# Products of all row elements, 1 core: the input loaded as seven units ahead and nine in one mid-run transfer, in place of seven loads spread over the start and mid-run

## The chip, the cores and the metric

The kernel runs on one core of a Trainium2 chip. The metric is the device time in microseconds (us), median of several executions. Before the change it is 1261.65 us, the median of 3 runs (1261.52 to 1261.91).

## What is computed

For each of 4096 rows of 256 float32 values, all products of two elements of the row with the second index not below the first, 32,896 values a row:

```
def reference(r_inputs):                       # (4096, 256) float32
    dot = jnp.einsum('bi,bj->bij', inputs, inputs)
    iu, ju = jnp.triu_indices(256)
    return dot[:, iu, ju]                      # (4096, 32896) float32
```

The output has 539 MB, the input 4.2 MB: the kernel writes 128 times what it reads.

## The kernel before, in words

**Tiles.** The 4096 rows lie on 128 partitions, 32 consecutive rows on each. Two rows of every partition make a *unit* (2 KB a partition, 256 KB in all), so the input has 16 units, numbered 0 to 15, and all of it stays in one tile `x`. A unit's output is cut into three parts of 10,944 to 11,008 columns; one part of one unit is a *piece*, 48 in all, written by one store of some 11 MB. `PASS = 6` pieces (two units) make a pass; the loop variable `h` counts the 8 passes and `p` the piece within a pass. Pieces 0 and 1 are made ahead of the loop, by VectorE with ScalarE (`scalar`, line 297) and, for piece 1, GpSimd.

**Stages.** Two output places `o` are used in turn (`PLACES = 2`). For each piece VectorE (`vector`, line 225; L275) makes most of the products, each instruction one or two runs of consecutive columns for both rows, and GpSimd (`gpsimd`, line 341; L360) the last part, up to an estimated 19.4 us (`BUDGET`). VectorE's first instruction of a piece waits until the store of the piece two before has landed (`free`), and releases GpSimd (`go`); its last one waits for GpSimd (`g_done`) and releases the store (`v_done`). SyncE (`sync`, line 380; L392) issues the stores in order, all on one queue. At the first piece of each unit VectorE copies the unit from `x` to `xv` and `xp` (L252, L254), from which both engines then read.

**The head.** Piece 0 is stored in five parts (`FIRST`, cuts at columns 704, 1984, 3968 and 6592), each as soon as ScalarE (L303) and VectorE (L236) have made it, so that stores begin early. TensorE only waits until all five have landed, then hands the place on (line 447).

**Loads.** SyncE issues three ahead of everything (lines 429 to 432): unit 0, then units 3, 4, 7 and 8 in one transfer, then unit 12. GpSimd issues the rest. Once unit 0 is there it loads units 1, 2, 5 and 6 (`EARLY`) in four transfers of 42, 42, 42 and 2 partitions, combed over the partitions (lines 438 to 445). In pass `h = 2`, after its part of piece `p = 2`, that is the fifteenth piece, it loads units 9 to 11 and 13 to 15 (`LATE`) in transfers of 100, 3 and 25 partitions (`late`, line 329); at `p = 5` of that pass it waits for them. Between these loads stand *marks*: transfers of 256-byte pieces of so many input rows (`STEPS`, `SKIP`) to a tile `marks` that nothing reads. What they have to do with the loads is worked out in the prediction.

## Time and profile before

| what | value |
|---|---|
| median of 3 runs | 1261.65 us |
| the profiled execution, its own time | 1261.66 us |
| its span (first to last instruction) | 1259.9 us |
| VectorE, GpSimd, ScalarE busy | 792.5, 800.1, 27.1 us |
| DMA: moved, mean rate | 543.25 MB, 431 GB/s |
| SyncE's queue / GpSimd's queue | 540.54 MB / 2.64 MB |
| DMA packets under 512 B | 1466 of 15,847 |

How to read it. The profile shows the DMA engines of the core as one line of tenths and one of GB/s; the transfer records behind it list every packet with its start, its duration, its size and its queue, but not the engine that carried it. An instruction's idle time stands before it, with what ended that idle time. The profiled execution's own time agrees with the median of the runs within 0.01 us, and lies 1.76 us above its span.

### The profile page before, as it was taken

Reading aid. Unit: us, or ns where it says so; the run is one execution under the profiler, and the core shown is the slowest. Engines: PE = TensorE matmul, PEld = TensorE weight load, DVE = VectorE, ACT = ScalarE, POOL = GpSimd, SP = SyncE. Lnnn points to the kernel's source line nnn. Section 1 sums busy time; section 2 is a strip of 40 time slices with the busy share of each in tenths; the row PEclk is TensorE's granted clock in tenths of the full one; section 3 lists DMA queues with packets and bytes.
Section 4 is the critical chain, followed back from the end, with each engine's and each line's share of the span. In section 5 each row is a group of like instructions: output and inputs, shape, how many; then the busy total and the mean of one; then the engine's idle time right before and its main releaser. Section 6 shows DMA issues by size and latency. Waiting matters only on the chain. (4 is left out here: it accounts for less than half of the span.)

```text
span 1259.9 us, 2787 instructions
## 1 busy us (share of the span) xinstructions
DVE 792.5 (63%) x1256; ACT 27.1 (2%) x74; POOL 800.1 (64%) x1124
## 2 busy tenths in 40 slices
DVE  8656746667475674766647666486655866468560
ACT  8000000000000000000000000000000000000000
POOL 7477674776666766477665775567656676566750
DMA  9999999999999999999999999999999999999999
GB/s 375 441 427 441 429 437 431 434 434 434 436 433 428 435 435 431 435 428 438 430 438 430 439 428 438 430 438 431 434 436 431 437 431 436 429 436 429 440 428 395
DMA packets 15847, 543.25 MB, mean 431 GB/s; under 512 B 1466, under 2 KB 1504, under 8 KB 3296
## 3 DMA queue, kind: packets, MB, share of 16 engines
q1 hardware_dynamic: 14704, 540.54, 99.3%
q0 software_dynamic: 1136, 2.64, 0.6%
q14 instruction: 7, 0.06, 0.0%
HBM read 4.21 MB, written 538.97 MB: 431 GB/s over the span
## 5 line engine op out<-in xcount | busy, mean ns | idle before, releaser
L360 POOL TENSOR_TENSOR o<-xv 128x696 f32<-128x696 f32 (+33 forms) x1105 | 791.1, 756 | 416.8 <-DVE o L275 416.5
L275 DVE TENSOR_TENSOR o<-xv,xp 128x588 f32<-128x588 f32 (+4 forms) x1195 | 761.1, 712 | 430.3 <-DMA out_dram<-o 195.3
L303 ACT ACTIVATE o<-x 128x198 f32<-128x198 f32 (+34 forms) x72 | 25.5, 447 | 0.8 <-DMA x<-in_r_inputs_dram 0.8
L254 DVE COPY xp<-x 128x512 f32 x15 | 10.3, 688 | 0.0
L236 DVE TENSOR_TENSOR o<-x,xp 128x470 f32<-128x470 f32 (+18 forms) x19 | 9.7, 585 | 0.0
L236 DVE TENSOR_TENSOR o<-x 128x510 f32<-128x510 f32 (+9 forms) x10 | 5.7, 646 | 2.5 <-DMA x<-in_r_inputs_dram 2.5
L252 DVE COPY xv<-x 128x512 f32 x15 | 6.4, 427 | 0.5
L327 POOL DMA_DIRECT2D x<-in_r_inputs_dram x7 | 4.5, 649 | 1.6 <-DMA x<-in_r_inputs_dram 1.6
L321 POOL DMA_DIRECT2D marks<-in_r_inputs_dram x6 | 3.6, 602 | 1.2 <-SPq L175 1.2
L346 POOL MEMSET xv<- 128x1 f32 x1 | 0.1, 93 | 2.1 <-POOLq L188 2.1
L435 ACT ACT_TABLE_LOAD x1 | 1.3, 1283 | 1.2 <-ACTq L188 1.2
L433 DVE MEMSET edge<- 128x32 f32 x1 | 0.1, 85 | 1.0 <-SPq L175 1.0
L232 DVE COPY xp<-x 128x512 f32<-128x512 f32 x1 | 0.7, 684 | 0.0
L347 POOL COPY xv<-x 128x512 f32<-128x512 f32 x1 | 0.6, 609 | 0.0
L435 ACT ACTIVATE edge<-edge 128x1 f32<-128x1 f32 x1 | 0.3, 296 | 0.0
L471 POOL MEMSET const-float32-0.0<- 128x1 f32 x1 | 0.1, 98 | 0.2 <-issue 0.2
L471 POOL MEMSET const-bfloat16-1.0<- 128x1 bf16 x1 | 0.1, 101 | 0.0
L471 POOL MEMSET const-uint8-127<- 128x1 uint8 x1 | 0.1, 101 | 0.0
L471 POOL MEMSET const-float32-1.0<- 128x1 f32 x1 | 0.1, 98 | 0.0
## 6 DMA issues: line engine op xcount, KB each, us to landing
out_dram<-o SPq DMA_DIRECT2D x31, 10944.0 KB, 32.9
out_dram<-o SPq DMA_DIRECT2D x16, 11008.0 KB, 31.2
out_dram<-o SPq DMA_DIRECT2D x1, 4352.0 KB, 18.6
out_dram<-o SPq DMA_DIRECT2D x1, 2624.0 KB, 13.8
out_dram<-o SPq DMA_DIRECT2D x1, 1984.0 KB, 11.8
out_dram<-o SPq DMA_DIRECT2D x1, 1280.0 KB, 9.9
x<-in_r_inputs_dram POOLq DMA_DIRECT2D x1, 1200.0 KB, 39.7
x<-in_r_inputs_dram SPq DMA_DIRECT2D x1, 1024.0 KB, 5.2
```

The costliest lines, as they stand in the source:

```text
L232: nc.vector.tensor_copy(xp, x_of(h, 0)).then_inc(v_own, 1)
L236: ins = nc.vector.tensor_tensor(place[:, :, at - lo : at - lo + length], window(x_of(h, 0)[:, j:], [[d, REPEAT], [1, 1], [1, length]]), wi ...
L252: ins = nc.vector.tensor_copy(xv[:, :each], x_of(h, p // PIECES))
L254: nc.vector.tensor_copy(xp, x_of(h, p // PIECES)).then_inc(v_own, 1)
L275: ins = nc.vector.tensor_tensor(place[:, :, at : at + m * length], window(xv[:, j:], [[d, REPEAT], [1, m], [1, length]]), window(xp[:, i:] ...
L303: nc.scalar.activation(places[p][:, r, at - lo : at - lo + length], xa[:, r * d + j : r * d + j + length], AF.Copy, scale=xa[:, r * d + i ...
L321: nc.gpsimd.dma_start(marks[lo:hi, :, :MARK], of).then_inc(marked, 16)
L327: nc.gpsimd.dma_start(to, of).then_inc(far, 16)
L347: nc.gpsimd.tensor_copy(xv[:, :each], x_of(0, 0)).then_inc(g_own, 1)
L360: ins = nc.gpsimd.tensor_tensor(place[:, :, at : at + m * length], window(xv[:, j:], [[d, REPEAT], [1, m], [1, length]]), window(xv[:, i:] ...
L435: nc.scalar.activation(edge[:, :1], edge[:, 1:2], AF.Copy, scale=edge[:, 2:3])
L471: nc = _bacc.Bacc("TRN2", target_bir_lowering=False, num_devices=1)
```

## The change

SyncE now loads unit 0 in two transfers, one for each of a partition's two rows, and then units 1 to 6 in one transfer of 12 KB a partition. GpSimd loads nothing at the start. In pass `h = 2`, ahead of its part of piece `p = 5` (the eighteenth piece), it issues a mark of 5 rows, a load of units 7 to 15 for partitions 0 to 119, a mark of 2 rows, and the same load for partitions 120 to 127: 18 KB a partition. It waits for them ahead of piece `p = 2` of pass 3. Since the first half of unit 0 can be there alone, VectorE's first instruction is split by row, and ScalarE does the first block row by row; each engine's first instruction on the second row waits for the second half. The counters that GpSimd and VectorE keep are carried on between the two halves of a pass in one way for both. The core of the diff:

```diff
-NEAR = [(0, 1, 1), (3, 7, 2), (12, 13, 1)]
-EARLY = (1, 5, 2)
-LATE = (9, 13, 3)
-WHEN = 2
-BEGUN, HAD = 2, 5
+NEAR = (1, 2, 3)
+LATE = (7, 3, 3)
+BEGUN, HAD = (2, 5), (3, 2)
-COMB = 3
-STEPS = (5, 2, 2, 12, 4)
-TENS, ODD, SKIP = 100, 3, 13
+MOST = 120
+STEPS = (5, 2)
...
-                    for i, j, at, length in block:
+                    todo = [(run, 0, REPEAT) for run in block]
+                    if c == 0:
+                        todo[:1] = [(block[0], r, 1) for r in range(REPEAT)]
+                    for (i, j, at, length), r, rows in todo:
...
+                        if r:
+                            ins._wait_ge(loaded[r], 16)
...
+                if p == c == 0:
+                    for r in range(1, REPEAT):
+                        todo[[of for _, of in order].index(r)]._wait_ge(loaded[r], 16)
...
     def late(h, p: int):
-        with nc.gpsimd.If(h == WHEN):
-            if p == BEGUN:
-                load(LATE, slice(0, TENS))
-                load(LATE, slice(TENS, TENS + ODD))
-                mark(0, SKIP)
-                load(LATE, slice(TENS + ODD, P))
-            else:
-                nc.gpsimd.wait_ge(far, 16 * (COMB + 4))
-                nc.gpsimd.wait_ge(marked, 16 * (COMB + 3))
+        if p == BEGUN[1]:
+            with nc.gpsimd.If(h == BEGUN[0]):
+                at = 0
+                for step, rows in zip(STEPS, (slice(0, MOST), slice(MOST, P))):
+                    mark(at, at + step)
+                    at += step
+                    to, of = units(LATE, rows)
+                    nc.gpsimd.dma_start(to, of).then_inc(far, 16)
+        if p == HAD[1]:
+            with nc.gpsimd.If(h == HAD[0]):
+                nc.gpsimd.wait_ge(far, 16 * len(STEPS))
+                nc.gpsimd.wait_ge(marked, 16 * len(STEPS))
                 nc.gpsimd.drain()
...
-    for (one, two, units), sem in zip(NEAR, loaded):
-        dims = [[(two - one) * each, 2 if two - one > units else 1], [1, units * each]]
-        to, of = (window(ap[:, one * each :], dims) for ap in (flat, x_in))
-        nc.sync.dma_start(to, of).then_inc(sem, 16)
+    for r in range(REPEAT):
+        part = slice(r * d, (r + 1) * d)
+        nc.sync.dma_start(flat[:, part], x_in[:, part]).then_inc(loaded[r], 16)
+    nc.sync.dma_start(*units(NEAR, slice(0, P))).then_inc(loaded[REPEAT], 16)
...
-    at = 0
-    for k, step in enumerate(STEPS):
-        if k == 1:
-            nc.gpsimd.wait_ge(loaded[0], 16)
-        if k:
-            load(EARLY, slice(k - 1, k + COMB * (teeth - 1), COMB) if k <= COMB else slice(P - rest, P))
-        mark(at, at + step)
-        at += step
-
+    nc.gpsimd.wait_ge(loaded[0], 16)
+    nc.gpsimd.wait_ge(loaded[1], 16)
```

More of the change, by code (lines that the diff above doesn't have):

```diff
@@ L181 @@
     head, v_done, a_done, go = (semaphore(s) for s in ("head", "v_done", "a_done", "go"))
-    loaded = [semaphore(f"loaded{k}") for k in range(len(NEAR))]
+    loaded = [semaphore(f"loaded{k}") for k in range(REPEAT + 1)]
     far, marked = semaphore("far"), semaphore("marked")
-    teeth = P // COMB
-    rest = P - COMB * teeth
     def take(engine, sem, value: int):
@@ L234, in vector @@
                         copied = done
-                    for i, j, at, length in block:
+                    todo = [(run, 0, REPEAT) for run in block]
+                    if c == 0:
+                        todo[:1] = [(block[0], r, 1) for r in range(REPEAT)]
+                    for (i, j, at, length), r, rows in todo:
+                        left = xp if c >= DIRECT else x_of(h, 0)
                         ins = nc.vector.tensor_tensor(
-                            place[:, :, at - lo : at - lo + length],
-                            window(x_of(h, 0)[:, j:], [[d, REPEAT], [1, 1], [1, length]]),
-                            window(xp[:, i:] if c >= DIRECT else x_of(h, 0)[:, i:], [[d, REPEAT], [1, 1], [0, length]]),
+                            place[:, r : r + rows, at - lo : at - lo + length],
+                            window(x_of(h, 0)[:, r * d + j :], [[d, rows], [1, 1], [1, length]]),
+                            window(left[:, r * d + i :], [[d, rows], [1, 1], [0, length]]),
                             ALU.mult,
                         )
+                        if r:
+                            ins._wait_ge(loaded[r], 16)
                         if copied:
@@ L300, in scalar @@
         for p in pieces:
-            for _, _, block, _, lo in blocks(p, True):
+            for c, (_, _, block, _, lo) in enumerate(blocks(p, True)):
+                order = [(run, r) for run in block for r in range(REPEAT)]
+                if p == c == 0:
+                    order.sort(key=lambda of: of[1])
                 todo = [
@@ L308, in scalar @@
                     )
-                    for i, j, at, length in block
-                    for r in range(REPEAT)
-                ]
+                    for (i, j, at, length), r in order
+                ]
+                if p == c == 0:
+                    for r in range(1, REPEAT):
+                        todo[[of for _, of in order].index(r)]._wait_ge(loaded[r], 16)
                 if todo:
@@ L321, in mark, with units, gpsimd @@
         nc.gpsimd.dma_start(marks[lo:hi, :, :MARK], of).then_inc(marked, 16)
-    def load(of_units: tuple, rows: slice):
-        one, two, units = of_units
-        dims = [[(two - one) * each, 2], [1, units * each]]
-        to, of = (window(ap[rows, one * each :], dims) for ap in (flat, x_in))
-        nc.gpsimd.dma_start(to, of).then_inc(far, 16)
-    def late(h, p: int):
-        with nc.gpsimd.If(h == WHEN):
-            if p == BEGUN:
-                load(LATE, slice(0, TENS))
-                load(LATE, slice(TENS, TENS + ODD))
-                mark(0, SKIP)
-                load(LATE, slice(TENS + ODD, P))
-            else:
-                nc.gpsimd.wait_ge(far, 16 * (COMB + 4))
-                nc.gpsimd.wait_ge(marked, 16 * (COMB + 3))
+    def units(of_units: tuple, rows: slice) -> tuple:
+        one, parts, of_part = of_units
+        dims = [[of_part * each, parts], [1, of_part * each]]
+        return tuple(window(ap[rows, one * each :], dims) for ap in (flat, x_in))
+    def late(h, p: int):
+        if p == BEGUN[1]:
[10 more added lines that the diff above has]
+                nc.gpsimd.wait_ge(marked, 16 * len(STEPS))
                 nc.gpsimd.drain()
-    def gpsimd(h, pieces: range, ahead: bool):
-        done = turns = 0
+    def gpsimd(h, pieces: range, ahead: bool, done: int = 0, turns: int = 0) -> tuple:
         if ahead:
@@ L353, in gpsimd @@
             turns += not ahead
+            if not ahead:
+                late(h, p)
             order = interleave(block)
@@ L373, in gpsimd @@
             ins.then_inc(g_done, 1)
-            if p in (BEGUN, HAD) and not ahead:
-                late(h, p)
-        nc.gpsimd.sem_inc(g_own, -done)
-        if turns:
-            nc.gpsimd.sem_inc(go, -turns)
+        return done, turns
     def sync():
@@ L396, in sync, with settle @@
             nc.sync.sem_inc(sem, -count)
-    def settle(counts: tuple):
-        for sem, count in zip((v_own, g_done), counts):
-            nc.vector.sem_inc(sem, -count)
+    def settle(engine, counts: tuple):
+        for sem, count in zip((v_own, g_done) if engine is nc.vector else (g_own, go), counts):
+            if count:
+                engine.sem_inc(sem, -count)
     def all_pieces(engine, pieces_of):
-        by_vector = engine is nc.vector
-        counts = pieces_of(0, range(AHEAD), True)
-        if by_vector:
-            settle(counts)
-        for sem in loaded[1:]:
-            engine.wait_ge(sem, 16)
-        engine.wait_ge(far, 16 * (COMB + 1))
-        engine.wait_ge(marked, 16 * (COMB + 2))
+        settle(engine, pieces_of(0, range(AHEAD), True))
+        engine.wait_ge(loaded[REPEAT], 16)
         kind = engine.engine
@@ L420, in all_pieces @@
                 nxt = nc.s_assert_within(h + 1, 0, passes - 1)
-                if by_vector:
-                    settle(vector(nxt, range(AHEAD), False, *counts))
-                else:
-                    pieces_of(nxt, range(AHEAD), False)
-        if by_vector:
-            nc.vector.wait_ge(v_own, counts[0]).then_inc(v_done, 1)
-            settle(counts)
-    for (one, two, units), sem in zip(NEAR, loaded):
-        dims = [[(two - one) * each, 2 if two - one > units else 1], [1, units * each]]
-        to, of = (window(ap[:, one * each :], dims) for ap in (flat, x_in))
-        nc.sync.dma_start(to, of).then_inc(sem, 16)
+                settle(engine, pieces_of(nxt, range(AHEAD), False, *counts))
+        if engine is nc.vector:
+            nc.vector.wait_ge(v_own, counts[0]).then_inc(v_done, 1)
+        settle(engine, counts)
+    for r in range(REPEAT):
+        part = slice(r * d, (r + 1) * d)
+        nc.sync.dma_start(flat[:, part], x_in[:, part]).then_inc(loaded[r], 16)
+    nc.sync.dma_start(*units(NEAR, slice(0, P))).then_inc(loaded[REPEAT], 16)
     nc.vector.memset(edge, 0.0).then_inc(warm, 1)
```

## The prediction

> **What bounds the kernel now.** I read the page's busy shares, its slices and its DMA queues first.

> ```profile
> DVE 792.5 (63%) x1256; ACT 27.1 (2%) x74; POOL 800.1 (64%) x1124
> DMA  9999999999999999999999999999999999999999
> q1 hardware_dynamic: 14704, 540.54, 99.3%
> q0 software_dynamic: 1136, 2.64, 0.6%
> ```

> No engine is over 64% busy; the DMA engines are full in every slice. By stretches (second column: length in us; last two: DMA share, GB/s):

> ```profile
> 0.00:2.00 2.00, 0.09 (x1) 0.78 (x1) 0.60 (x5) 1.00 0.03 3
> 2.00:4.00 2.00, 0.36 (x1) 1.16 (x3) 0.42 (x2) 1.00 0.92 298
> 6.00:8.00 2.00, 2.00 (x4) 2.00 (x7) 2.00 (x4) 1.00 0.98 318
> 430.00:1240.00 810.00, 518.07 (x821) 0.00 (x0) 521.37 (x739) 1.00 1.00 434
> ```

> The first packet runs at 1.98 us; from there to the end something is always moving. The waits agree: the compute engines wait for stores or for each other, with room.

> ```profile
> POOL o L360 <- DVE o L275: 416.5, 46, 12.6
> DVE o L275 <- DMA out_dram<-o: 195.3, 31, 9.1
> ```

> So the time is the start (2 us), the work of the most loaded of 16 DMA engines, and its idle time. Only those three can move it. The transfer records show the work: a packet is followed by the next 4 ns before its recorded end, so I can follow each engine from packet to packet. Every store closes with 16 four-byte completions, one per engine. Their times, relative to the first (us):

> ```
> piece 1  : 0.00 1.11 1.24 1.28 1.33 1.38 1.49 1.59 1.68 1.73 1.81 1.87 1.96 2.14 2.29 2.70
> piece 12 : 0.00 0.04 0.04 0.09 0.14 0.24 0.35 0.44 0.49 0.52 0.57 0.63 0.72 0.90 1.05 1.86
> piece 15 : 0.00 1.79 2.81 2.86 2.91 3.56 3.61 3.65 3.68 3.76 3.83 3.87 3.96 4.00 4.08 4.14
> piece 47 : 0.00 1.02 1.06 1.12 1.77 1.82 1.86 1.89 1.97 2.04 2.08 2.16 2.21 2.25 2.29 2.35
> ```

> The last engine ends 0.61 us after the mean of piece 47: perfect balance would gain only that. Three engines are odd. One **drifts**: 1.24 us ahead of the pack's front at piece 1, level at 12, ahead by 2.81 after the late load, 1.2 behind the same neighbours at 47; that is 0.11 to 0.126 us a store, about 5.9 us in all (its packets are stretched by 4 to 33 ns now and then). Two others, A and B, lose about 2.05 and 1.3 us before piece 12, around six of the 8 KB instruction packets (queue 14) between 31 and 140 us.

> **The rule.** [...] of the 256 late packets of 6144 bytes, the chains that I can follow cleanly carry 20 or 21, one none, as 100 rows on ten engines give. [...] From cursor 0, before: mark 5 moves it to 5, each load of 42 rows takes 14 engines (3 rows each) and leaves out 3 and 4; late, 100 rows take 5 to 14 (10 rows each), 3 rows take 15, 0, 1, mark 13 passes over 2 to 14, 25 rows take 15, 0 to 3 (5 rows each). Engine 4 gets no GpSimd load and 3 and 2 little: the drifter is 4, the one with most lead at piece 15; A is 3 and B 2, which fits the 1.79 (A) and a level B. Afterwards: mark 5, then 120 rows on 15 engines, 8 rows each, leaving out 4; mark 2 passes 4 and 5; 8 rows fall on 6 to 13. So 4 gets nothing, 0 to 3, 5, 14, 15 eight rows, 6 to 13 nine.

> **Prices.** Net per packet (recorded less 4 ns): 2 KB 80 ns, 4 KB 155, 6 KB 230. The line through these gives 43 ns for 1 KB, 455 for 12 KB, 680 for 18 KB. Bounds for 18 KB: the same slope (680), or three packets of 6 KB (690): 0.1 us over nine rows. For 1 KB: 43 to 80, 0.6 us over 16.

> **Part by part, on one engine.**
> 1. SyncE's loads: before 16x80 + 16x155 = 3.76 us; after 16x43 + 8x455 = 4.32 (+0.56).
> 2. Early GpSimd loads, gone: 3 transfers x 3 rows x 2 x 155 = 2.79 us on the full engines.
> 3. Late load: before 20x230 = 4.60; after nine rows 6.12, or eight 5.44.
> 4. Marks and completions of GpSimd's 13 transfers: about 0.3 us; of 4, about 0.1.

> Full engine before: 3.76+2.79+4.60+0.3 = 11.45. After, 6 to 13: 4.32+6.12+0.1 = 10.54 (-0.91). Engine 3 (A): 4.32+5.44+0.1+2.05 = 11.91 (**+0.46**); no early load is withheld from it any more. Engine 2: 11.16. Drifter: 4.32+0.1+5.9 = 10.32. So A ends last.

> 5. Idle at the start. Early loads covered it: the trace shows two engines without them (3 and 4) idle from 6.75 to 7.21 and from 8.95 to 9.56 us, waiting for the first two head stores, which were issued at 4.83 and 6.69 and first moved 2.4 and 2.9 us later. Afterwards all 16 are like these two. But their loads end 0.56 later (7.3), and the head is earlier: half of unit 0 is issued at the same 0.96, has half the bytes, and lands by about 3.2 instead of 3.64; the second, issued some 0.45 later, by about 3.5. VectorE's first instruction (cadence 0.61) becomes two of 0.34, hidden under those waits; then store 1 can go at about 4.4. If the second half lands late (4.1), store 1 goes at 5.0. New idle time: between 0 (stores early) and 1.05 (the whole idle time of those two engines); between the two halves another 0 to 0.2. I take 0.2.
> 6. A's place in the pack: the ten full engines end spread over 0.6 us and the last counts; A alone takes a middle place: -0.3.
> 7. GpSimd's four issues (2.5 us from 364.40 to 367.06 now) move before the eighteenth piece, into the 8.64 us that it waits there anyway; before, they stood in a wait of 9.35.

> ```profile
> 364.40 1.43 POOL L327 DMA_DIRECT2D x<-in_r_inputs_dram  x2
> 366.39 0.67 POOL L327 DMA_DIRECT2D x<-in_r_inputs_dram  x1
> 376.41 18.21 POOL L360 TENSOR_TENSOR o<-xv 128x924 f32<-128x924 f32 x14 [9.35 <-DVE o L275]
> 431.02 14.71 POOL L360 TENSOR_TENSOR o<-xv 128x292 f32<-128x292 f32 x39 [8.64 <-DVE o L275]
> ```

> Behind them on GpSimd stands only that piece; SyncE's queue shares engines, not instructions. The load gets a packet in turn with a store packet (8 x 2.3 = 18 us) and has until the twenty-second piece, some 100 us. The wait for it at piece 2 of pass 3 finds it landed: nothing. The wait for units 1 to 6, ahead of the loop, too.
> 8. Stores are issued some 3.7 us before an engine runs dry (issue 451.11, its first packet 1.0 later, pieces of 25.8 us). The drifter, freed of loads, would lead A by about 5.8 and is stopped at 3.7; with 29 stores x 0.12 = 3.5 still to lose it ends about level with A. No cost, but no reserve either.

> Sum: +0.46 +0.2 -0.3 = +0.4 us on the profiled execution (1261.66; the median is the same within 0.01): **1262.0 us**. A measurement of this kernel tells some 0.2% (2.5 us) from no change, so I call this no change.

> **Rivals.**
> - *The instruction packets fall elsewhere or at other times* (the program is shorter), so that A is no outlier. Then 6 to 13 end last: -0.91+0.2 = -0.7: **1260.9**. For: nothing ties those packets to engine 3 but one trace. Against: the engines' loops stay as they are. 28 in 100.
> - *The head stores come late and all engines idle* as the two did: +0.46+1.05-0.1 = **1263.1**. For: the same wait is in the trace. Against: the stores should come 0.4 earlier and the loads last 0.56 longer. 13 in 100.
> - *The skipped place isn't the drifter's.* If 120 rows are dealt otherwise (16 engines, or another cursor), the drifter carries eight or nine rows: 4.32+5.44+5.9+0.1 = 15.8, +4.3 against 11.45, +0.2: **1266.1**, slower. It decides from the sixth row on the drifter. For: [...] engine numbers aren't recorded. Against: the same walk explains who leads at piece 15. 6 in 100.
> - *Faster by more than 0.2%*: mean work falls only from 10.24 to 9.83 us an engine (all load packets over 16), and 0.61 of imbalance is there; 1.0 together. 2 in 100.

> The forecast has 49; 2 remain for a slowdown that I don't see. Range 1260.4 to 1263.8: it takes in the forecast, the first two rivals and the bounds of steps 1 and 5. Faster 0.02, within 0.2% 0.90, slower 0.08.

> **What would show it.** Records: 256 packets of 1 KB (near 46 ns), 128 of 12 KB (near 460) and 128 of 18 KB (near 684); no GpSimd DMA before 360 us; four issues near 422 us and no longer idle time ahead of the next VectorE piece. Completions at the last piece: one engine last, alone, by about 1.4 us, and the drifter near it. First store issued near 4.4. It is wrong if some engine ends over 2 us after the others (the cursor), if slices after the first fall below 427 GB/s (stores dry), or if the first slice falls below 370 (idle start).

## The result, and the profile after

| | median, us | ratio to before, 95% interval |
|---|---|---|
| before | 1261.61 (6 runs) | |
| the changed kernel | 1267.35 (6 runs) | 1.0044 [1.0031, 1.0057] |

The change makes the kernel 5.7 us slower. The forecast was 1262.0 within 1260.4 to 1263.8, no change; the measured time lies nearest to the third rival (1266.1, or 1266.8 with nine rows on the drifter). The profiled execution took 1267.38 us, its span is 1265.6.

The page of the changed kernel, busy shares, slices and queues:

```profile
DVE 792.9 (63%) x1257; ACT 27.2 (2%) x74; POOL 795.4 (63%) x1115
DMA  9999999999999999999999999999999999999997
GB/s 377 434 442 430 435 436 429 439 426 440 425 441 430 419 437 427 438 431 436 432 435 432 433 437 428 439 426 427 439 428 437 427 440 426 439 426 440 426 440 340
q1 hardware_dynamic: 14576, 540.81, 99.0%
q0 software_dynamic: 240, 2.36, 0.5%
```

The compute engines are as busy as before. What is new is at the right edge: the last slice drops to a 7 and 340 GB/s. Short stretches of the changed kernel around its end (columns as above; next to last the share of 16 engines that moves something):

```profile
1256.00:1258.00 2.00, 0.00 (x0) 0.00 (x0) 0.00 (x0) 1.00 1.37 594
1258.00:1260.00 2.00, 0.00 (x0) 0.00 (x0) 0.00 (x0) 1.00 0.26 110
1260.00:1262.00 2.00, 0.00 (x0) 0.00 (x0) 0.00 (x0) 1.00 0.05 22
1262.00:1264.00 2.00, 0.00 (x0) 0.00 (x0) 0.00 (x0) 1.00 0.05 22
```

A share of 0.05 is one 44 KB packet in two microseconds: one engine of 16 works alone. (Packets count where they start, so a share can be over 1.) The same stretches before end together:

```profile
1256.00:1258.00 2.00, 0.00 (x0) 0.00 (x0) 0.00 (x0) 1.00 0.61 264
1258.00:1260.00 2.00, 0.00 (x0) 0.00 (x0) 0.00 (x0) 1.00 0.00 0
```

The completions of single stores in the changed kernel, one per engine, relative to the first (us), from its transfer records:

```
piece 12 : 0.00 0.09 0.09 0.12 0.19 0.19 0.23 0.24 0.25 0.40 0.44 0.57 1.10 1.54 1.61 2.41
piece 16 : 0.00 4.84 5.05 5.22 5.22 5.42 5.52 5.62 5.70 5.78 7.00 7.22 7.51 7.79 8.20 8.30
piece 18 : 0.00 0.64 0.85 1.01 1.02 1.21 1.31 1.41 1.50 1.58 2.79 3.02 3.31 3.58 4.10 4.16
piece 37 : 0.00 0.00 0.06 0.07 0.08 0.08 0.10 0.11 0.13 0.15 0.60 0.83 1.12 1.40 1.91 4.39
piece 47 : 0.00 0.00 0.01 0.02 0.06 0.07 0.07 0.07 0.08 0.10 0.11 0.14 0.15 0.24 0.75 4.36
```

The drifter is the 1.61 of piece 12. The late load makes one engine lead by 4.84 us, but the drifter is now at the other end (8.2): it wasn't left out. The leader finds no store to go on with and stands still for 4.2 us, which is why it is back at 0.64 ahead at piece 18. From then on the drifter is last, everybody's next store waits for it, and the others close up at 4.0 to 4.4 us ahead of it, again at every third store. In the middle of the run the engines are idle for 1.60 us on average (0.02 before).

The compute side shows it as one long wait after the load. Changed kernel, the pieces after it, and then the kernel before at the same place:

```profile
426.17 20.11 DVE L276 TENSOR_TENSOR o<-xv,xp 128x260 f32<-128x260 f32 x41 [8.20 <-DMA out_dram<-o]
458.40 13.24 DVE L276 TENSOR_TENSOR o<-xv,xp 128x1024 f32<-128x1024 f32 x14 [11.05 <-DVEq L183]
459.70 18.23 POOL L368 TENSOR_TENSOR o<-xv 128x924 f32<-128x924 f32 x14 [18.26 <-DVE o L276]
```

```profile
456.28 4.49 DVE L275 TENSOR_TENSOR o<-xv,xp 128x1024 f32<-128x1024 f32 x4 [4.60 <-DVEq L188]
```

VectorE waits 11.05 us instead of 4.60 for the store two pieces back (piece 16 of the table), all 16 engines of it. In the waits of the whole run little else changes:

```profile
POOL o L368 <- DVE o L276: 421.7, 46, 18.3
DVE o L276 <- DMA out_dram<-o: 195.4, 31, 8.2
DVE o L276 <- DVEq L183: 82.0, 14, 11.1
```

The last of these lines before:

```profile
DVE o L275 <- DVEq L188: 74.3, 14, 5.8
```

The end of the last data moves from 1258.23 to 1263.86 us, by 5.63. The mean end of the 16 engines moves by 2.26: 1.58 more idle time in mid-run, 0.61 more **stretch** of store packets (the time that a packet takes beyond the 1.62 us, or 1.63 for the larger ones, of most store packets), 0.73 more in load packets, 0.41 less in head stores. These add to 2.5; the 0.25 less is mostly in small packets, of which there are fewer. The other 3.37 is imbalance: the last engine ends 3.98 us after the mean instead of 0.61, and 3.61 after the next one, the sign that the prediction had named for a wrong cursor.

### The profile page after: what moved, and what is told of

The parts are those of the page before. It is cut to its first block, busy times and chain, and to the rows that moved or that the text cites. A ratio compares the mean times of both kernels' runs of the same rounds, so it can differ in the third digit from the quotient of the medians.

```text
span 1265.6 us, 2763 instructions
## 1 busy us (share of the span) xinstructions
DVE 792.9 (63%) x1257; ACT 27.2 (2%) x74; POOL 795.4 (63%) x1115
## 5 line engine op out<-in xcount | busy, mean ns | idle before, releaser
L235 DVE TENSOR_TENSOR o<-x 128x255 f32<-128x255 f32 (+9 forms) x11 | 5.9, 599 | 2.0 <-DMA x<-in_r_inputs_dram 1.9
L327 POOL DMA_DIRECT2D marks<-in_r_inputs_dram x2 | 1.4, 702 | 0.0
L342 POOL DMA_DIRECT2D x<-in_r_inputs_dram x2 | 1.1, 554 | 0.0
```

The source lines that it names most:

```text
L235: ins = nc.vector.tensor_tensor(place[:, r : r + rows, at - lo : at - lo + length], window(x_of(h, 0)[:, r * d + j :], [[d, rows], [1, 1], ...
L327: nc.gpsimd.dma_start(marks[lo:hi, :, :MARK], of).then_inc(marked, 16)
L342: nc.gpsimd.dma_start(to, of).then_inc(far, 16)
```

## The experiments

The prediction's walk has each GpSimd transfer go on at the engine behind the last one that the transfer before used (the *cursor*). The records of before fit it for the late load: 20 of its 256 packets on each of ten engines, 12 on each of three, 10 on each of two and none on one, and one packet of the mark of 13 rows on every engine but the three with 12. That the new load goes the same way was my estimate; no trace of before shows a load of its form.

Theory 1, drawn from these completions: rows of *one* run (18 KB, contiguous) aren't dealt from the cursor. They go in blocks from engine 0: 120 rows fill 0 to 14 with eight each and leave out 15, the 8 rows go one each to 0 to 7. The records of the changed kernel fit it already. Counting per engine, the seven engines that carried a row of a mark (0 to 6) are engines with nine late rows; an eighth has nine and no mark, seven have eight, and the leader has neither. Had the cursor dealt the loads, the marks would lie on 0 to 5 and the nine rows on 6 to 13: no marked engine would carry nine. The rival, theory 2: the cursor deals as forecast, and the drifter sits elsewhere.

**The first mark longer.**

```diff
-STEPS = (5, 2)
+STEPS = (9, 2)
```

> As the changed kernel, but the first mark has 9 rows instead of 5. Theory 1: a GpSimd transfer whose rows are one run each isn't dealt from the cursor; it is dealt in blocks of ceil(rows/16) from engine 0, so 120 rows fill 0 to 14 and leave out 15, and 8 rows fall on 0 to 7, whatever the marks do. Then nothing moves: 1267.3 us (within 0.4), one engine leads all others by about 5 us after the late load as before, the drifting engine ends 3.6 us after the next. Theory 2: the cursor rule of the prediction holds, and the drifter only sits in another place. Then 120 rows leave out the engine four places on and the eight rows go to others: for most places of the drifter it now carries eight rows instead of nine (1266.7), for one it carries none (1262).

1267.24 us, 1.0043 [1.0028, 1.0059]: the time doesn't move. The records show eight engines with nine rows, all of them marked, three marked ones and four unmarked with eight, and the leader without mark: marks on 0 to 10 and rows dealt from 0, as theory 1 has it. From the cursor the left-out engine would have been number 8, which is marked. One part of the expectation missed: the leader is ahead by only 1.88 us after the load, not by about 5. Four of its store packets took 2.16 to 2.19 us beside the load, and its stretch in all is 2.8 us; the leader of the changed kernel, left out of the same rows in the same way, had 0.03 us. The time doesn't show this, since the drifter ends last.

**Two runs a row.** The late load takes units 7 to 10 and 12 to 15.

```diff
-                    to, of = units(LATE, rows)
+                    to, of = (window(ap[rows, LATE[0] * each :], [[5 * each, 2], [1, 4 * each]]) for ap in (flat, x_in))
...
+    nc.sync.dma_start(*units((11, 1, 1), slice(0, P))).then_inc(loaded[REPEAT], 16)
```

> As the changed kernel, but the late load takes units 7 to 10 and 12 to 15, two runs of 8 KB a row, and SyncE loads unit 11 at the start. Rows and marks are the same (120 and 8, marks of 5 and 2). Theory 1 (rows of two runs are dealt from the cursor, rows of one run are not): engine 4, the drifter, gets nothing, and the time comes back to 1261 to 1262.5 (A last: 4.32 + 0.64 for unit 11 + 8 x 0.605 + 2.05 + 0.1 = 11.95 against 11.45 before, +0.5; with the start and A's place as predicted 1262.0). Theory 2 (the drifter sits elsewhere, the form of the rows has no part): as the changed kernel, 1267 +- 0.7.

1264.87 us, 1.0021 [1.0012, 1.003]: 2.5 us faster than the changed kernel, and not the 1262 that theory 1 expected. The records have both answers. The packets per engine are 18 on eight engines, 16 on seven, none on one; that one carries a row of *each* mark, as only engine 4 does in the walk (mark 0 to 4, load 5 to 3, mark 4 and 5), and it was 2.18 us behind before the load: the drifter. So rows of two runs are dealt from the cursor, and the drifter was left out. But while the others loaded, its own store packets took for some 20 us 1.78 to 2.08 us instead of 1.62: 3.57 us of stretch in all, zero on 14 of the other engines and 0.13 on one. Of 4.9 us that the left-out engine should have won, 1.3 were left. It ended alone again, 2.0 us after the next, while the mean end of the 16 engines is that of before (1257.57 against 1257.62 us). The last stretches of this run, shorter by one packet than in the changed kernel:

```profile
1256.00:1258.00 2.00, 0.00 (x0) 0.00 (x0) 0.00 (x0) 1.00 0.26 110
1258.00:1260.00 2.00, 0.00 (x0) 0.00 (x0) 0.00 (x0) 1.00 0.05 22
1260.00:1262.00 2.00, 0.00 (x0) 0.00 (x0) 0.00 (x0) 1.00 0.00 0
```

**One load of 128 rows.** No marks, no second transfer.

```diff
-                for step, rows in zip(STEPS, (slice(0, MOST), slice(MOST, P))):
-                    mark(at, at + step)
-                    at += step
+                for rows in (slice(0, P),):
...
```

> As the changed kernel, but the late load is one transfer of 128 rows of 18 KB and there are no marks: every engine carries eight rows, the drifter too. If the drifter's ninth row is what the last 8-row transfer costs: 0.68 us less, 1266.6, and the drifter still ends alone, by about 3.6 us (before: nine rows on it and on A and B). If the slowdown came from the start, or from the waits of the late load, and not from the drifter's rows: 1267.3 or above, without one engine ending alone.

1265.68 us, 1.0029 [1.0018, 1.0041], 1.7 faster than the changed kernel; the drifter ends alone by 3.63 us (1261.60 against 1257.97). The ninth row is 0.7 of it. The rest is stretch: here each load packet took 686 ns on average, in the changed kernel 739 (up to 1022), and hardly a store packet beside the load is stretched, against 0.6 us an engine on average there. The stretches 422 to 450 us of the changed kernel, of this run, and of the one with two runs a row, in that order:

```profile
422.00:450.00 28.00, 21.14 (x43) 0.00 (x0) 14.75 (x39) 1.00 1.00 418
```

```profile
422.00:450.00 28.00, 21.14 (x43) 0.00 (x0) 14.74 (x39) 1.00 1.01 438
```

```profile
422.00:450.00 28.00, 21.14 (x43) 0.00 (x0) 14.71 (x39) 1.00 0.99 425
```

The share is 1 in all three; the rate tells them apart. A busy engine can be a slow one.

**The kernel before, with one run a row.** Of the kernel before, only the late load is changed; it takes unit 12 as well, which SyncE loaded ahead.

```diff
-NEAR = [(0, 1, 1), (3, 7, 2), (12, 13, 1)]
-LATE = (9, 13, 3)
+NEAR = [(0, 1, 1), (3, 7, 2)]
+LATE = (9, 16, 7)
...
-        dims = [[(two - one) * each, 2], [1, units * each]]
+        dims = [[(two - one) * each, 2 if two - one > units else 1], [1, units * each]]
```

> As the kernel before, but the late load takes units 9 to 15 in one run of 14 KB a row (unit 12 no longer by SyncE), still 100, 3 and 25 rows with the mark of 13 between; start and place of the load as before. Theory 1: 100 rows are dealt seven to an engine from 0, 3 and 25 rows again from 0: engine 4 carries 7 + 2 = 9 rows of 0.53 = 4.8 us instead of none. Drifter: 3.12 + 0.3 + 4.8 + 5.9 and 1.0 idle at the start = 15.1 against 11.45: 1265.3, slower than before with the old start. Theory 2: the form of the rows does nothing; 11.45 less 0.64 for unit 12 plus 10 rows x 0.53 less 4.6 = +0.06: 1261.6.

1265.41 us, 1.0027 [1.0016, 1.0038], within 0.1 us of what theory 1 expected. One engine ends 2.9 us after the next. In the records one engine carries no row, one two and one seven, as 100 rows dealt seven to an engine from engine 0 leave them. The form of the rows makes the old kernel slower, with nearly the old start and the old place of the load. It isn't their size: rows of 14 KB in one run ignore the cursor here, rows of 16 KB in two runs followed it above.

**Left out twice.** Two runs a row, dealt so that A and B carry five rows, the drifter none and the others nine; the last partition is loaded by SyncE.

```diff
-STEPS = (5, 2)
+STEPS = (5, 3)
-zip(STEPS, (slice(0, MOST), slice(MOST, P)))
+zip(STEPS, (slice(0, 52), slice(52, P - 1)))
...
+    to, of = (window(ap[P - 1 : P, LATE[0] * each :], [[5 * each, 2], [1, 4 * each]]) for ap in (flat, x_in))
+    nc.sync.dma_start(to, of).then_inc(loaded[REPEAT], 16)
```

> As the run with two runs a row, but dealt to balance the three odd engines: 52 rows on 13 engines (2, 3 and 4 left out), a mark of 3, 75 rows on 15 (4 left out), the last partition by SyncE at the start: nine rows on most, five on A, none on the drifter. Theory 1 (the stores of a left-out engine are stretched as long as the others load, which eats the lead it should have won): the drifter again wins little over one us and ends alone, 1264.9 within 0.6. Theory 2 (the stretch in that run was an accident of its row order): no engine ends late, 10.5 us of load work against 11.45, 1260.9.

1264.58 us, 1.0021 [1.0013, 1.0029]. In the profiled execution (1263.44, one of the fastest) the drifter, with no load packet, has 2.97 us of stretch, the two engines with five rows 1.14 and 1.56, the others 0 to 0.45. This fits what the run was to show, that an engine that carries less than its neighbours has its stores stretched while they load. It isn't a rule: the leader of the changed kernel carried nothing and had none.

**The start alone.** The new start with the old late load.

```diff
-BEGUN, HAD = (2, 5), (3, 2)
+BEGUN, HAD = (2, 3), (2, 5)
-LATE = (7, 3, 3)
+LATE = (9, 13, 3)
...
+    nc.sync.dma_start(*units((7, 1, 2), slice(0, P))).then_inc(loaded[REPEAT], 16)
+    nc.sync.dma_start(*units((12, 1, 1), slice(0, P))).then_inc(loaded[REPEAT], 16)
```

> The start of the changed kernel with the late load of the one before (units 9 to 11 and 13 to 15, two runs a row, 100, 3 and 25 rows with a mark of 5 and 13, after the fifteenth piece); units 7, 8 and 12 by SyncE at the start. Theory 1 (the early loads mattered because engines 3 and 4 were left out of them, which gave the drifter 1.8 us of lead): the drifter ends last, 6.2 + 5.9 + 0.8 = 12.9 against 11.45, 1263.1. Theory 2 (the start has no part in the slowdown, only the form of the late load has): full engines 6.2 + 4.6 + 0.1 = 10.9, 1261.1 to 1261.6.

1263.91 us, 1.0016 [1.0009, 1.0022], nearer to theory 1, but mostly for another reason. The drifter doesn't end alone: it ends level with another engine (2.31 and 2.33 us after the first). The mean end is 1.07 us later than before, because the load packets took 12.26 us an engine instead of 11.06: SyncE's 12 KB packets 549 ns on average, its 4 KB ones 262, where I had 455 and 155, and the late 6 KB ones 271 (before 234). So the new start costs some 2 us together with the two loads added here; how much of it is its own stays open.

**Engine 3 left out.** Two runs a row.

```diff
-STEPS = (5, 2)
+STEPS = (4, 2)
```

> As the run with two runs a row, but the first mark has 4 rows instead of 5, so that the load of 120 rows leaves out engine 3 (A) and not the drifter. If the cursor deals rows of two runs and the drifter is engine 4: it now carries eight rows (4.9 us) with its stores unstretched, instead of none with 3.57 us of stretch: 1.3 us more than that run, 1266.2; the stretched engine is another, A. If the stretch belongs to engine 4 itself and not to the left-out place: it has both, 1269.

1266.43 us, 1.0034 [1.0021, 1.0047], as expected from the cursor and the drifter's place (1266.2). The drifter carries eight rows and has some 0.3 us of stretch beside the load, so the stretch of the other runs doesn't belong to that engine itself, which would have given 1269. Around the load the packets of the left-out engine and of another can't be told apart, so on which of these the stretch fell isn't shown.

**Other partitions at other times.** As two runs a row, the big load on partitions 4 to 123.

```diff
-STEPS = (5, 2)
+STEPS = (5, 2, 0)
...
-zip(STEPS, (slice(0, MOST), slice(MOST, P)))
+zip(STEPS, (slice(4, 4 + MOST), slice(0, 4), slice(4 + MOST, P)))
...
```

> As the run with two runs a row, but the big load takes partitions 4 to 123 instead of 0 to 119 (the other eight in two transfers of 4 rows, on the same eight engines): same engines, same bytes, same drifter left out; only which partitions are written when is moved by four. In the run before, the left-out engine's 18 store packets beside the load ran unstretched for the first two rows of each engine, by 440 to 460 ns for the next two and by 230 to 270 for the last four. Theory P [...]: the pattern moves along the load, stretched at the start and free of it later. Theory Q (the stretch comes with the place in the transfer, whatever is written): the first two rows are free again. Both: about 1264.9, the drifter last.

1263.68 us, 1.0012 [1.0006, 1.0019]. The drifter's stretch falls to 2.2 us, 1.4 less than with partitions 0 to 119, and the median by 1.2: in these two, stretch and time go together. Its place fits neither theory. It begins at 438.7 us instead of 431.9 and lasts to the end of the load, mostly at 240 to 320 ns a packet, without the packets stretched by some 450 ns. Whether the partitions made this difference isn't shown: each kernel has one trace, the two ran on different chips, and with the same rows dealt in the same numbers (nine on eight engines, eight on seven, none on one) the stretch of the left-out engine was 0.03 us in the changed kernel and 2.8 with the longer mark.

## Why the prediction was wrong

**The step that failed: how the rows are dealt.** I put the walk beside the trace of *before*, where it fits, and carried it to a load of another form. Every GpSimd load before has two runs a row, and the late one's counts (20, 12, 10 and no packets an engine) fit a cursor; the new one has one run of 18 KB, a form that the trace of before doesn't hold. The longer mark (nine rows on marked engines alone), the two-runs run (none on the engine with a row of each mark) and the old kernel with one run a row (no row on one engine, two on one, seven on one) settle it for these loads: one-run rows ignore the cursor, two-run rows follow it. So "4 gets nothing" was wrong: the drifter got nine rows. My rival had the price: 1266.8 with nine, measured 1267.35. I gave it 6 in 100 because the walk explained who leads at piece 15; that was evidence on the old form alone.

**A second step failed once the first was mended:** that a left-out engine wins all that it doesn't carry. With the drifter left out the time is 1264.87, not 1262.0. I had priced a store packet beside a load like one alone; in that run it took up to 2.08 us instead of 1.62, 3.57 us in all, and on the drifter, the one engine that can't afford it. The trace of before had a sign of it: its left-out engine had some 0.8 us of stretch beside the late load, which I did not price. But it doesn't follow from being left out alone, as the 0.03 us of the changed kernel's leader show.

The cause of the stretch is not shown. In one load of 128 rows there is next to none (438 GB/s over 422 to 450 us, against 418 in the changed kernel). With the shifted rows it fell from 3.57 to 2.2 us, but began later and lasted to the end of the load, as neither theory had it; and the changed kernel and the longer mark, with the same rows dealt to the engines in the same numbers, differ by 2.8 us on the left-out engine.

**By the steps.**
1. SyncE's loads: 1 KB packets had a median of 46 ns, as forecast, but the 12 KB ones 490 and a mean of 645; only the fastest had the line's 460. With the halves that is 5.9 us an engine, not 4.32. (The loads of before were dearer than their price too, 4.4 instead of 3.76, so the change is +1.5, not +0.56.)
2. and 4., the loads and marks that go: as forecast, GpSimd moves nothing before 417 us.
3. 18 KB: 689 ns median against 684. The mean of 739 has stretch in it; the drifter's nine rows took about 7.1 us, not 6.12.
5. The start: right. Half of unit 0 lets both engines begin at 3.02 us (before 3.64), the first store goes at 4.47 (forecast 4.4), and from the first packet to 30 us the engines are idle for about 0.5 us on average, in both kernels.
7. GpSimd's issues: right; they lie in a wait that is 6.83 us long after them, and nobody waits for GpSimd longer than before (VectorE 6.3 us at most in both kernels).

```profile
3.02 5.97 DVE L235 TENSOR_TENSOR o<-x 128x255 f32<-128x255 f32 x11 [1.90 <-DMA x<-in_r_inputs_dram]
4.47 4.92 SPq L396 DMA_DIRECT2D out_dram<-o  x3
417.36 0.81 POOL L327 DMA_DIRECT2D marks<-in_r_inputs_dram  x1
426.68 14.75 POOL L368 TENSOR_TENSOR o<-xv 128x292 f32<-128x292 f32 x39 [6.83 <-DVE o L276]
```

8. The limit on a lead was there (forecast 3.7, measured 4.0 to 4.4), with the sides changed: the drifter is the slow end, so the limit holds back the 15 others and costs 1.6 us on average.

Of step 6: A's place no longer mattered: with nine rows A ended within 0.75 of the rest, since the others were waiting for the drifter.

None of the eight variants is faster than the kernel before.

## What to carry to other kernels

Where the transfer engines are the bound, balance is counted per engine, and a change in the *form* of a transfer (two runs a row merged into one) can change which engines carry it without changing a byte (the drifter, left out of the late load before, got nine rows of the new one): count packets per engine in the records before a rule is carried from one form to another. A share of 100% doesn't say that an engine runs at its rate; GB/s in the same stretch does (418 at a share of 1.00, 438 at 1.01). An engine spared a load can win less than the load's length (1.3 of 4.9 us with two runs a row), because its other packets may slow down beside it (up to 2.08 us instead of 1.62); whether they do is read from the records of the run itself.
